# Layer norm statistics from VectorE's batch-norm instruction in a two-layer graph kernel

## The chip, the cores and the metric

The kernel runs on one core of a Trainium2 chip. The core has five engines that run side by side, each working through its own queue of instructions in order: TensorE (PE in the profile), VectorE (DVE), ScalarE (ACT), GpSimd (POOL) and SyncE (SP, which issues plain DMA transfers). They wait for one another through semaphores. The metric is the device time of one execution in microseconds (us), as the median of several runs.

## The reference

Sixteen graphs (B) of 1024 nodes (N) with 64 channels (C) each go through two layers. Each layer starts with a layer norm over the channels and a ReLU.

```python
def _layernorm(x, axis=-1, eps=1e-5):
    m = jnp.mean(x, axis=axis, keepdims=True)
    v = jnp.var(x, axis=axis, keepdims=True)
    return (x - m) / jnp.sqrt(v + eps)

# layer 0
h = jnp.maximum(_layernorm(x), 0.0)
x = x + matmul(adj / clip(sum(adj, 2), 1), h)
# layer 1
h = jnp.maximum(_layernorm(x), 0.0)
x = x + L1(h, adj, nodemask, W1, b1, W2, b2)
```

Layer 1 looks at the neighbours of every node (the nonzero entries of its row of `adj`), leaves out some of them in nodes with more than ten neighbours, takes three quantiles of the neighbours' values in each channel, adds their weighted sum to the node's own value, and sends the result through a small two-layer network of 128 hidden units.

## The kernel before

A batch is one graph. Its 1024 nodes lie as 8 row blocks (NT) of 128 partitions (P), so that a tensor of node features is a tile of 128 x 8 x 64.

The program is written by a planner that runs on the host while the instructions are issued. Each kind of work is a Python generator, called a stream. Before each step it yields the engine that it needs next and a function that says when its data will be there by the planner's own clocks. `Plan.run` takes the stream that can begin earliest (with a rank to put one before another) and lets it issue up to its next yield. `Plan.note` (line 271) advances the clocks: it prices a VectorE operation at 0.07 us plus 1.04 ns per element of the largest operand, a ScalarE operation at 0.06 us plus 0.86 ns per element, 0.11 us for each per-partition operand and 0.09 us for an accumulated output, and an indirect DMA at 1.27 us. So the order of instructions on every engine depends on the planner's prices, while the chip runs each engine's queue in that order, whatever the real times are. The margins SLACK (2 us), LOOSE (7 us) and LATE (14 us) keep a step from being put too early.

Layer 0 is made of eight streams (lines 560 to 809), each of which runs over the 16 batches:

- `loads` brings the node features `xt` and the rows `at` of the adjacency by SP's DMA queue; `signs` makes `sg`, the signs of a row block, on ScalarE, and `listing` takes the largest eight of four segments of them on VectorE (`rec`), which are the neighbour lists.
- `beginnings` (line 578) does the first layer norm: it calls `normed` (line 504) on `xt` and writes `h0`, the input of the products.
- `transposes` turns the adjacency on TensorE, and ScalarE copies it out (`att`); `products` multiplies it by `h0` and adds the residual on VectorE, which writes the layer's result into `row[:, :, X1:R0]`.
- `channels` (line 723) does the second layer norm: it calls `normed` on that part of `row`, writes the first 64 columns of `row`, and has SP store them in the table `tab`.
- `endings` sorts the nodes by their number of neighbours and scatters the records (`row`) to `srt` with eight indirect DMAs per batch, which GpSimd issues.

When the four batches of a group are done, `group` (line 1102) prepares the group's lists on VectorE, and jobs follow (`Job`, line 831): each gathers neighbours' rows from `tab` into `places` by indirect DMAs on GpSimd (four buffers), sorts them by min and max on VectorE, weights them on ScalarE and VectorE, sums and multiplies on TensorE, and scatters the result to the output, again from GpSimd. The jobs of the first three groups run in between layer 0 of later batches. After layer 0 come the last group and the jobs of the longest lists (`long_lists`, tiles `lplaces` and `long_other`).

`normed` is what the change touches. It takes `xt`, an input of 128 x 8 x 64. One VectorE reduction sums each row of 64, and one operation scales the eight sums to minus the mean (`s`). Then ScalarE squares each of the eight blocks with `s` as its bias, and the accumulated output of each square is a column of `v`, the sum of squared deviations. A yield stands before every second square (line 512), so other streams' ScalarE work can come between; another (line 517) puts VectorE's next step 2 us after the last square. VectorE scales `v` and adds epsilon, ScalarE takes the square root, VectorE the reciprocal and the product with `s`, and ScalarE applies scale, bias and ReLU to the eight blocks in `h`. A second path, `dense_path`, with its own `normed`, is taken only if the lists overflow.

Of the kernel before, what the change touches and what calls it, by code (L numbers as in the profile page):

```python
# [9 lines left out]
F32 = mybir.dt.float32  # L10
# [4 lines left out]
AF = mybir.ActivationFunctionType  # L15
OP = mybir.AluOpType
AX = mybir.AxisListType

P = 128
# [195 lines left out]
SLACK = 2.0  # L215
# [18 lines left out]
class Plan:  # L234
# [25 lines left out]
    def room(self, name, bufs):  # L260

        tiles = self.slots.get(name, ())
        if len(tiles) < bufs:
            return 0.0
        old = tiles[-bufs]
        return INF if self.users[old] else max(self.used.get(old, 0.0), self.ready.get(old, 0.0))

    def at(self, *tiles):
        return max(self.ready.get(t.tensor.name, INF) for t in tiles)
# [104 lines left out]
def list_path(ctx, tc, x, adj, nodemask, w1, b1, w2, b2, out, go):  # L374
    nc = tc.nc
    B, N, C = x.shape
    H = w1.shape[1]
    CO = w2.shape[1]
    NT = N // P
# [8 lines left out]
    X1 = W  # L388
    R0 = X1 + C
# [9 lines left out]
    tiny = ctx.enter_context(tc.tile_pool(name="tiny", bufs=2))  # L399
# [98 lines left out]
    nc = plan.nc  # L498
    new, free, room, at = plan.tile, plan.release, plan.room, plan.at
# [1 line left out]

    def normed(h, xt):

        s = new(tiny, [P, NT], F32, "ln_s", 4)
        nc.vector.tensor_reduce(s, xt, AX.X, OP.add)
        nc.vector.tensor_scalar(s, s, -1.0 / C, None, op0=OP.mult)
        v = new(tiny, [P, NT], F32, "ln_v", 4)
        for t in range(NT):  # L510
            if t % 2 == 0:
                yield "ACT", lambda: at(s)
            sq = new(tiny, [P, C], F32, "ln_sq", 2)
            nc.scalar.activation(
                sq, xt[:, t, :], AF.Square, bias=s[:, t:t + 1], accum_out=v[:, t:t + 1]
            )
        yield "DVE", lambda: at(v) + SLACK
        nc.vector.tensor_scalar(v, v, 1.0 / C, EPS, op0=OP.mult, op1=OP.add)
        yield "ACT", lambda: at(v) + SLACK
        nc.scalar.activation(v, v, AF.Sqrt)  # L520
        yield "DVE", lambda: at(v) + SLACK
        nc.vector.reciprocal(v, v)
        nc.vector.tensor_tensor(s, s, v, OP.mult)
        for t in range(NT):
            if t % 2 == 0:
                yield "ACT", lambda: at(s)
            nc.scalar.activation(
                h[:, t, :], xt[:, t, :], AF.Relu, bias=s[:, t:t + 1], scale=v[:, t:t + 1]
            )
# [26 lines left out]
    def known(st, *names):  # L556

        return max(at(st[name]) if name in st else INF for name in names)
# [19 lines left out]
    def beginnings(pool, now):  # L578

        for b, st in enumerate(batch):  # L580
            now[0] = b
            yield "DVE", lambda: max(known(st, "xt", "mrow"), room("h0", 3), room("row", 4))
            mrow_f = new(tiny, [NT, P], F32, "mrow_f", 2)
            nc.vector.tensor_copy(mrow_f, st["mrow"])

            h0 = new(pool, [P, NT, C + 1], F32, "h0", 3, users=2)
            nc.vector.memset(h0[:, :, C:], 1.0)
            row = st["row"] = new(pool, [P, NT, RW], F32, "row", 4, users=1)
            nc.vector.memset(row[:, :, C:W], -1.0)
            yield from normed(h0[:, :, :C], st["xt"])  # L590
            st["h0"] = h0
            yield "PE", lambda: max(at(mrow_f), room("ps_small", 3))
            pm = new(ps_s, [P, HALF], F32, "ps_small", 3, users=1)
            nc.tensor.transpose(pm[:, :NT], mrow_f, ident[:NT, :NT])
            yield "ACT", lambda: at(pm)
            nc.scalar.copy(row[:, :, RW - 1], pm[:, :NT])
            nc.scalar.copy(row[:, :, RW - 2], row_f)
            free(pm)
# [124 lines left out]
    def channels(pool, now):  # L723

        for b, st in enumerate(batch):
            now[0] = b
            row = lambda: st["row"]
            yield "DVE", lambda: known(st, "row") if st["residual"] == 2 else INF
            yield from normed(row()[:, :, :C], row()[:, :, X1:R0])
            g = max(g for g in range(NG) if FIRST[g] <= b)  # L730
            lo = (b - FIRST[g]) * TS
            nc.sync.dma_start(
                tabs[g][lo:lo + N, :].rearrange("(t p) w -> p t w", p=P), row()[:, :, :W]
            )
            st["normed"] = True
# [592 lines left out]
    with tc.tile_pool(name="lay0", bufs=2) as pool:  # L1328

        for stream, first in (  # L1330
            (endings, 0), (channels, 1), (products, 2), (transposes, 4), (listing, 5),
            (beginnings, 6), (loads, 7), (signs, -15),
        ):
            now = [0]
            plan.add(stream(pool, now), lambda first=first, now=now: 10 * now[0] + first)
        plan.run(lambda: progress["batches"] == B)
# [5 lines left out]
    nc = tc.nc  # L1342
# [291 lines left out]
```

## Time and profile before

| what | value |
|---|---|
| median of 3 runs | 1947.84 us (1942.62 to 1948.89) |
| span of the profiled execution, first to last instruction | 1511.0 us |
| mean granted TensorE clock in it | 0.699 of full speed |
| median less span | 436.8 us |
| DMA | 133.36 MB, mean 88 GB/s |
| ScalarE busy with the squares and their accumulator reads (`ln_sq`) | 34.02 us before 216 us, 55.91 us from there to 890 us |

The profile comes from one execution and gives the span alone; its whole time is not listed, so the difference to the median of other runs stands beside it. Busy time counts a moment once, even where two instructions of an engine overlap in the pipeline, so it is less than the count times the mean duration. "Idle before" is time in which an engine did nothing before an instruction of that group, and what ended it is named after an arrow. All instructions that the planner issues carry line 228 (its helper), so groups are told apart by the tile that they write: `ln_s`, `ln_v` and `ln_sq` are the layer norms, `row` the records, `srt` their scatter, `places` and `lplaces` the gathered neighbours, `y` and `out_dram` the output.

### The profile page before, as it was taken

The numbers are of one execution on the slowest core, as the hardware profiler recorded it, in microseconds if no ns is written. First come the engines' busy times: TensorE is split into PE (matmuls) and PEld (weight loads), VectorE is DVE, ScalarE is ACT, GpSimd is POOL, SyncE is SP. The second block draws the span as 40 slices with busy tenths as digits, with TensorE's granted clock in tenths as the row PEclk, the third lists the DMA queues.
The fourth block names the chain that finished last, engine by engine and source line by source line (L and its number), as shares of the span: only waits on it lengthen the run. The fifth ranks groups of instructions, "written<-read, shape, count | busy, mean of one in ns | idle before, by whom it ended". The sixth has DMA issues, their size and how long they took to land. (4 is left out here: it accounts for less than half of the span.)

```text
span 1511.0 us, 15983 instructions
## 1 busy us (share of the span) xinstructions
PE 738.8 (49%) x3192; PEld 464.7 (31%) x3192; DVE 1191.3 (79%) x4104; ACT 816.4 (54%) x2789; POOL 957.2 (63%) x1154
## 2 busy tenths in 40 slices
PE   4778777327877556567667620024000123228542
PEld 2434334214544233343444320012000122216432
DVE  6777798997899779859869869893059999986875
ACT  7989878557879457757975520201050223148341
POOL 0122227777678757757777787667777777765083
PEclk8889888658888777869688755555555565558765
DMA  5445665424355253355341242111111111211010
GB/s 177 150 142 168 163 210 160 123 73 114 101 162 152 59 174 94 99 126 161 94 140 31 60 101 68 50 37 28 30 26 23 28 28 40 44 33 22 2 25 13
DMA packets 135718, 133.36 MB, mean 88 GB/s; under 512 B 100756, under 2 KB 103444, under 8 KB 135492
## 3 DMA queue, kind: packets, MB, share of 16 engines
q1 hardware_dynamic: 102876, 90.79, 20.8%
q0 software_dynamic: 32736, 41.47, 11.2%
q14 instruction: 78, 0.64, 0.1%
q8 instruction: 28, 0.46, 0.1%
HBM read 112.90 MB, written 23.61 MB: 90 GB/s over the span
## 5 line engine op out<-in xcount | busy, mean ns | idle before, releaser
L228 POOL DMA_INDIRECT places<-tab,idx x372 | 370.2, 995 | 131.7 <-issue 101.8
L228 PE MATMUL pt<-ident,prod 128*128 128x128 f32 (+1 forms) x736 | 160.2, 377 | 517.8 <-DVE prod L228 241.2
L228 PEld LDWEIGHTS pt<-ident,prod 128*128 128x128 f32 (+1 forms) x736 | 129.3, 256 | 550.4 <-ACT prod L228 412.4
L228 PE MATMUL ps_small<-att,h 128*65 128x512 f32 x512 | 254.7, 644 | 27.3 <-ACT h L228 10.5
L228 POOL DMA_INDIRECT srt<-row,to x128 | 125.9, 984 | 165.8 <-ACT row L228 144.0
L228 PE MATMUL pt<-ident,at 128*128 128x128 f32 x1024 | 176.7, 320 | 96.0 <-ACT att L228 71.1
L228 POOL DMA_INDIRECT lplaces<-whole,lidx x163 | 167.2, 1026 | 55.6 <-issue 48.5
L228 DVE MAX8 rec<-sg 128x8 f16<-128x256 f16 x512 | 180.1, 414 | 4.4
L228 PEld LDWEIGHTS pt<-ident,at 128*128 128x128 f32 x1024 | 136.9, 164 | 143.5 <-ACT att L228 93.8
L228 ACT ACTIVATE sg<-at 128x1024 f16<-128x1024 f32 x128 | 134.8, 1054 | 75.0 <-DMA at<-in_adj_dram 65.7
L228 ACT COPY att<-pt 128x512 f32<-128x512 f32 x256 | 141.9, 582 | 20.7 <-PE pt L228 18.8
L228 POOL DMA_INDIRECT places<-tab,last_idx x124 | 123.8, 998 | 41.3 <-issue 35.0
L228 PEld LDWEIGHTS ps_small<-att,h 128*65 128x65 f32 x512 | 74.7, 151 | 161.9 <-issue 123.2
L228 ACT ACTIVATE places<-places,gone 128x64 f32<-128x64 f32 x496 | 123.5, 335 | 0.5
L228 ACT ACTIVATE prod<-places,w 128x64 f32<-128x64 f32 x213 | 54.1, 336 | 120.5 <-DVE w L228 120.5
L228 POOL DMA_INDIRECT out_dram<-y,nodes_i x93 | 91.8, 987 | 22.6 <-issue 15.1
L228 DVE TENSOR_TENSOR sg<-sg,keyed 128x1024 f16<-128x1024 f16 x128 | 87.2, 681 | 23.7 <-ACT sg L228 23.7
L228 ACT ACTIVATE gone<-gone 128x15 f32<-128x15 f32 (+9 forms) x40 | 8.2, 206 | 169.2 <-DVE ok L228 169.0
L228 DVE TENSOR_TENSOR long_other<-lplaces 128x512 f32<-128x512 f32 (+5 forms) x124 | 64.1, 555 | 29.1 <-ACT lplaces L228 28.9
L228 DVE TENSOR_TENSOR other<-places,other 128x64 f32<-128x64 f32 (+6 forms) x204 | 69.6, 341 | 5.9
L228 PE MATMUL ps_small<-ot,w_sb 128*128 128x128 f32 (+3 forms) x112 | 47.6, 513 | 44.2 <-DVE y L228 31.2
L228 DVE TENSOR_TENSOR places<-places,other 128x64 f32<-128x64 f32 (+2 forms) x208 | 62.3, 309 | 4.9
(231 smaller groups left out, 1670.8 us busy)
## 6 DMA issues: line engine op xcount, KB each, us to landing
at<-in_adj_dram SPq DMA_DIRECT2D x128, 512.0 KB
places<-tab,idx POOLq DMA_INDIRECT x372, 2.5
whole<-tab SPq DMA_DIRECT2D x4, 1057.0 KB
tab<-row SPq DMA_DIRECT2D x16, 264.0 KB
xt<-in_x_dram SPq DMA_DIRECT2D x16, 256.0 KB
lplaces<-whole,lidx POOLq DMA_INDIRECT x163, 2.4
srt<-row,to POOLq DMA_INDIRECT x128, 2.7
places<-tab,last_idx POOLq DMA_INDIRECT x124, 2.4
```

What stands on the lines that cost most here:

```text
L228: ins = getattr(self._engine, op)(*args, **kwargs)
```

## The change

`normed` gets a switch `stats`, and both calls in layer 0 set it. With it, eight `bn_stats` instructions on VectorE, one for each block of 64 elements, write six numbers each: count, mean and sum of squared deviations of the elements with even index, and the same of those with odd index. Five further VectorE operations on 128 x 8 elements put the halves together: the difference of the two means (`apart`), their sum (`s`), the sum of the two squared deviations (`v`), then C/4 times the square of the difference, which is added to `v`. Minus one half times `s` is then minus the mean. The reduction, the eight squares on ScalarE, the yields before them and the yield after them are not issued on this path. From the scaling of `v` on nothing changes. `dense_path` is unchanged.

```diff
--- before.py
+++ after.py
@@ -501,20 +501,34 @@
 
 
 
-    def normed(h, xt):
+    def normed(h, xt, stats=False):
 
         s = new(tiny, [P, NT], F32, "ln_s", 4)
-        nc.vector.tensor_reduce(s, xt, AX.X, OP.add)
-        nc.vector.tensor_scalar(s, s, -1.0 / C, None, op0=OP.mult)
         v = new(tiny, [P, NT], F32, "ln_v", 4)
-        for t in range(NT):
-            if t % 2 == 0:
-                yield "ACT", lambda: at(s)
-            sq = new(tiny, [P, C], F32, "ln_sq", 2)
-            nc.scalar.activation(
-                sq, xt[:, t, :], AF.Square, bias=s[:, t:t + 1], accum_out=v[:, t:t + 1]
-            )
-        yield "DVE", lambda: at(v) + SLACK
+        if stats:
+            st = new(tiny, [P, NT, 6], F32, "ln_st", 2)
+            for t in range(NT):
+                nc.vector.bn_stats(out=st[:, t, :], in_=xt[:, t, :])
+            apart = new(tiny, [P, NT], F32, "ln_apart", 2)
+            nc.vector.tensor_tensor(apart, st[:, :, 1], st[:, :, 4], OP.subtract)
+            nc.vector.tensor_tensor(s, st[:, :, 1], st[:, :, 4], OP.add)
+            nc.vector.tensor_tensor(v, st[:, :, 2], st[:, :, 5], OP.add)
+            nc.vector.scalar_tensor_tensor(
+                apart, apart, float(C) / 4.0, apart, op0=OP.mult, op1=OP.mult
+            )
+            nc.vector.tensor_tensor(v, v, apart, OP.add)
+            nc.vector.tensor_scalar(s, s, -0.5, None, op0=OP.mult)
+        else:
+            nc.vector.tensor_reduce(s, xt, AX.X, OP.add)
+            nc.vector.tensor_scalar(s, s, -1.0 / C, None, op0=OP.mult)
+            for t in range(NT):
+                if t % 2 == 0:
+                    yield "ACT", lambda: at(s)
+                sq = new(tiny, [P, C], F32, "ln_sq", 2)
+                nc.scalar.activation(
+                    sq, xt[:, t, :], AF.Square, bias=s[:, t:t + 1], accum_out=v[:, t:t + 1]
+                )
+            yield "DVE", lambda: at(v) + SLACK
         nc.vector.tensor_scalar(v, v, 1.0 / C, EPS, op0=OP.mult, op1=OP.add)
         yield "ACT", lambda: at(v) + SLACK
         nc.scalar.activation(v, v, AF.Sqrt)
@@ -587,7 +601,7 @@
             nc.vector.memset(h0[:, :, C:], 1.0)
             row = st["row"] = new(pool, [P, NT, RW], F32, "row", 4, users=1)
             nc.vector.memset(row[:, :, C:W], -1.0)
-            yield from normed(h0[:, :, :C], st["xt"])
+            yield from normed(h0[:, :, :C], st["xt"], True)
             st["h0"] = h0
             yield "PE", lambda: max(at(mrow_f), room("ps_small", 3))
             pm = new(ps_s, [P, HALF], F32, "ps_small", 3, users=1)
@@ -726,7 +740,7 @@
             now[0] = b
             row = lambda: st["row"]
             yield "DVE", lambda: known(st, "row") if st["residual"] == 2 else INF
-            yield from normed(row()[:, :, :C], row()[:, :, X1:R0])
+            yield from normed(row()[:, :, :C], row()[:, :, X1:R0], True)
             g = max(g for g in range(NG) if FIRST[g] <= b)
             lo = (b - FIRST[g]) * TS
             nc.sync.dma_start(
```

## The prediction

> **What bounds the kernel now.** I read five views in this order: the page's busy shares and slices, the busy time in four stretches, the waits of GpSimd, the groups by shape on ScalarE, and the timeline of VectorE for durations. The page first:
>
> ```profile
> PE 738.8 (49%) x3192; PEld 464.7 (31%) x3192; DVE 1191.3 (79%) x4104; ACT 816.4 (54%) x2789; POOL 957.2 (63%) x1154
> ...
> DVE  6777798997899779859869869893059999986875
> ACT  7989878557879457757975520201050223148341
> POOL 0122227777678757757777787667777777765083
> ```
>
> By shares VectorE (DVE) looks like the bound, and the change loads it further. But the GpSimd row stays at 6 to 8 tenths from the sixth slice to the 36th, and that is a full queue: between two gathers lie 0.30 us that the waits view calls "issue", so a 0.99 us gather takes a 1.25 to 1.3 us turn. The stretches and GpSimd's waits in the first two of them:
>
> ```profile
> 0.00:216.00 216.00, 161.44 (x646) 83.54 (x646) 165.78 (x598) 183.94 (x560) 40.31 (x76) 0.87 0.54 164
> 216.00:890.00 674.00, 421.01 (x1759) 259.61 (x1760) 561.66 (x1955) 465.71 (x1574) 498.33 (x617) 0.75 0.41 114
> 890.00:1170.00 280.00, 31.18 (x121) 20.78 (x119) 183.57 (x609) 43.43 (x167) 210.32 (x224) 0.52 0.19 44
> 1170.00:1511.00 341.00, 125.20 (x668) 100.75 (x668) 280.30 (x944) 123.35 (x488) 208.22 (x239) 0.63 0.12 26
> ```
> ```profile
> POOL srt L228 <- ACT row L228: 134.7, 8, 63.7
> POOL tab L228 <- DVE deg L228: 17.3, 1, 17.3
> POOL gat_rows L228 <- DVE nodes_i L228: 16.3, 1, 16.3
> ```
> ```profile
> POOL places L228 <- issue: 87.8, 288, 0.3
> POOL gat_rows L228 <- DVE y L228: 12.3, 1, 12.3
> ```
>
> The columns of a stretch are its length, busy time of PE, PE's loads, DVE, ACT and POOL, the clock, the DMA share and GB/s. The reader is to see two regimes. Up to 216 us GpSimd starves: it waits 134.7 us for the ScalarE writes into `row`, then 34 us for the preparation of the first group. ScalarE is the busiest engine there (184 of 216 us). From 216 us GpSimd works through its queue with hardly a stop: in the next 674 us its real waits (12.3, 9.2, 7.1, 5.6 and a few of 2 us) make some 40 us. From 890 to 1170 us it waits some 10 us in all, and VectorE stands idle for 48.9 us at one go waiting for the gathers of the longest list. Only after 1170 us does it wait much again:
>
> ```profile
> POOL out_dram L228 <- DVE y L228: 58.1, 5, 36.2
> ```
>
> So the time is the moment at which GpSimd gets its first group, plus its queue, plus what it still waits.
>
> [...] the turn (start to start of operations that don't depend on each other): 29 maxima of 32 elements take 2.77 us, so (2.77 - 0.18)/28 = 92 ns[...]; the duration shown for one is some 85 ns longer, which a dependent one waits out. [...]
>
> **The change part by part**, per call of `normed` (32 calls: 16 batches times two norms).
>
> Removed from ScalarE: eight squares and their accumulator reads.
>
> ```profile
> L228 ACT ACTIVATE ln_sq<-xt,ln_s 128x64 f32<-128x64 f32 x128 | 42.8, 341 | 4.3 <-DVE ln_s L228 4.3
> ...
> L228 ACT ACTIVATE ln_sq<-row,ln_s 128x64 f32<-128x64 f32 x128 | 42.5, 334 | 11.9 <-DVE ln_s L228 11.9
> ```
>
> The reads overlap the squares (pairs follow at 0.33 us), and the windows of `ln_sq` have 34.0 us before 216 us, 55.9 after, together 89.9: 2.8 us per call.
>
> Removed from VectorE: the sum and its wait.
>
> ```profile
> 53.64 0.69 DVE L228 TENSOR_REDUCE ln_s<-row 128x8 f32<-128x512 f32 x1
> 54.36 0.17 DVE L228 TENSOR_SCALAR ln_s<-ln_s 128x8 f32<-128x8 f32 x1
> ```
>
> That is 0.72 us to the dependent scaling, which is 0.08 more to the next independent one; the scaling itself comes back with another factor.
>
> Added to VectorE: eight statistics of 64 elements. No row shows one. [...] I take 0.127[...]. Then, after 0.1 us for the dependence, five 8-element operations and the scaling: three independent at 0.08, two more links of the chain at 0.20 and 0.08, the scaling 0.08: 0.6 us. Together 1.7 us for 0.8: +0.9 us per call, +28 us in all, 11 in the first stretch (12 calls have their `ln_v` there) and 18 in the second. With dear statistics +2.7 us per call, +86 us.
>
> Moved: the wait of VectorE for the squares goes (3.9 us in the first stretch, 5.3 in the second), and one trip VectorE-ScalarE-VectorE per call. In the first batch the second norm runs from 53.64 to the first ReLU at 66.99, of which the squares take 57.6 to 61.5; the square root then stands behind a copy. The 14 operations leave in one piece, with nothing of another stream between: what is queued behind them on VectorE (mostly a sign product with four maxima, 2.1 us) is late by 1.7 us at most, and those waiting for it have buffers ahead (4 of `sg`). The planner prices a statistic at 0.07 + 64 x 0.00104 = 0.137 us, close to my value, so its order fits the engines as well as before. No DMA is added or moved in itself; the `row` scatters (8 on GpSimd) and the table store on SP follow their producer.
>
> *First stretch.* Between 60 and 180 us ScalarE is busy 107.7 of 120 us, TensorE 90, VectorE 88; batches follow at 32.8, 34.5 and 33.2 us (first `row` scatters at 67.7, 100.5, 135.0, 168.2). Two calls a batch take 5.6 us from ScalarE and give VectorE 1.8. ScalarE would then need some 25 us a batch, VectorE 26, TensorE 25, and none can be packed without gaps: I take 30 to 31, so 3 us for each of three batches. The first batch gains some 4 us through four calls less before it, and the preparation of the first group, on VectorE from 177 to 213 us, loses 2. That is 3 x 3 + 4 - 2 = 11, say 12 with the shorter trip of the last second norm. Bounds: 0, if DMA (0.54 busy) and TensorE keep the pace, to 20, all of the 34 us less 14 for VectorE and the gaps.
>
> *Second stretch.* VectorE gets 18 us and loses 10.2 us of waits inside the norms; its other waits for ScalarE (18.0 for gathered rows, 13.4 for signs) get shorter as ScalarE loses 56 us. I cost this at nothing: it is hidden under GpSimd's queue. Without that cover it would be up to 18 us.
>
> *The rest.* The code is the same, the stretch to 1170 us has 49 us of slack on VectorE, but the planner's order can differ.
>
> Sum: span 1511.0 - 12 = 1499. The page doesn't list the profiled execution's whole time; the median of the three runs lies 436.8 us above the span, and I leave that as it is: 1936.
>
> **Rivals.**
> *Nothing measurable (1944 to 1953, take 1947).* The start is earlier, but GpSimd runs into later `row`s and waits it out, or the end is set by the last long list on VectorE. For it: VectorE is busy for 192 of the 200 us from 1150. Against: GpSimd hardly waits between 216 and 1170.
> *The last drain turns out worse (slower, take 1960).* Near the end a scatter waits 36.2 us for `y` while the 20 gathers of the last long list stand behind it on GpSimd; they start at 1434 us and all that follows waits for them. The planner puts scatters and gathers in order by its own clocks, which the change shifts (ScalarE 2.5 us less per call, VectorE 0.9 more). If one more wait of this kind stands ahead of a long list's gathers, it costs 25 to 35 us; with the 12 gained, +12 to +20. It decides from a wait of some 20 us. For it: the tail has 58 us of such waits. Against: the same luck can take one away, to 1910.
> *Dear statistics (slower, take 1965).* At 0.35 us or more each, VectorE needs +54 us in the second stretch; 112 of its 674 us aren't busy, 73 of that in named waits, of which half can't go. It becomes the bound from some +35 us on; then the start's gain is gone too: about +17.
>
> **How the numbers follow.** Earlier start 0.50, nothing 0.16, worse drain 0.20, dear statistics 0.14. About 0.3%, 5.8 us, can be told from no change. Faster 0.50, same 0.16, slower 0.34. The likeliest case alone runs from 1920 (20 at the start and a kinder drain) to 1942. The range has to reach into both slower rivals: 1912 to 1968.
>
> **What would show it.** Right: no squares, ScalarE at about 727 us busy, VectorE near 1220, statistics at about 0.21 us each with a turn near 0.13; the first `tab` scatter some 12 us before 213; GpSimd's waits between there and 1170 unchanged near 50 us. Wrong: a turn of the statistics over 0.3 us; the first group no earlier; new GpSimd waits for `row` or for `places` on VectorE; or an end in which the long lists' gathers stand behind other waits.

## The result, and the profile after

The changed kernel takes 1949.4 us (median of 19 runs, 1936.2 to 1960.6), the kernel before takes 1950.9 us in as many runs beside it (1942.6 to 1957.7). The ratio is 0.9989 with a 95% interval of 0.9969 to 1.0008: no change that can be measured. The forecast was 1936 us; what came is the rival "nothing measurable".

One thing has to be known to read the numbers below. The same program ran in two lengths: the kernel before took about 1515 us in some sessions and about 1950 to 1980 us in others, on one and the same chip within half an hour, and never anything in between. The profile that the prediction argued from (span 1511.0 us) is of the short kind; all 19 + 19 timed runs of the result are of the long kind, and so is the profile of the changed kernel. Its span is 1942.5 us and the time of that same execution 1944.27 us, so the time around a span is some 2 us, not the 436.8 us that the prediction carried along. To compare like with like, the kernel before was profiled again in a long session (`b_again`, span 1954.5 us).

First the page of the changed kernel: busy time, share of the span and instructions, then the busy tenths in 40 slices.

```profile
PE 785.2 (40%) x3192; PEld 491.9 (25%) x3192; DVE 1219.7 (63%) x4487; ACT 748.1 (39%) x2295; POOL 943.1 (49%) x1155
...
DVE  7989649556643675774555738940025987646764
ACT  7786526254246453524652301001410142136341
POOL 0231662634652356475454456675773036573163
```

The work changed as foreseen: `b_again` has 1193.5 us for VectorE and 830.3 for ScalarE, so VectorE got 26.2 us more and ScalarE 82.2 less. But the GpSimd row, which stood at 5 to 8 tenths in the short profile from its seventh slice to its 37th, now swings between 2 and 7, with one slice at 0 and one at 1, and after the start no engine stays full: VectorE reaches 9 tenths in three slices, the others in none.

The statistics by tile in the changed kernel (duration in ns as min/median/max), and the timeline of VectorE in its first norm (start, length, operation):

```profile
L228 DVE BATCH_NORM_STATS2 ln_st<-xt x128: 193/197/229, 7.8 to 966.8; 128x6 f32<-128x64 f32 x128
L228 DVE BATCH_NORM_STATS2 ln_st<-row x128: 207/211/227, 58.6 to 1109.1; 128x6 f32<-128x64 f32 x128
```
```profile
7.78 1.07 DVE L228 BATCH_NORM_STATS2 ln_st<-xt 128x6 f32<-128x64 f32 x8
8.89 0.17 DVE L228 TENSOR_TENSOR ln_apart<-ln_st 128x8 f32<-128x8 f32 x1
...
9.54 0.17 DVE L228 TENSOR_SCALAR ln_v<-ln_v 128x8 f32<-128x8 f32 x1
```

Eight statistics take 1.07 us, and from the first of them to the scaling of `ln_v` it is 9.54 - 7.78 = 1.76 us, against the 1.7 of the prediction. The 0.35 us each of the rival "dear statistics" were a supposition of the author's; measured are 0.20 and 0.21 us for one, with a turn of (1.07 - 0.20)/7 = 0.124 us.

Now the stretches, with the same columns as before. The first two of the changed kernel, then the same of `b_again`:

```profile
0.00:216.00 216.00, 167.10 (x704) 90.46 (x704) 189.94 (x777) 167.09 (x396) 53.82 (x93) 0.89 0.63 187
216.00:890.00 674.00, 299.93 (x1166) 179.35 (x1166) 417.79 (x1598) 288.14 (x861) 351.48 (x431) 0.67 0.33 86
```
```profile
0.00:216.00 216.00, 152.49 (x586) 78.96 (x587) 153.37 (x565) 178.44 (x547) 38.25 (x73) 0.84 0.53 155
216.00:890.00 674.00, 339.80 (x1308) 207.05 (x1306) 410.65 (x1430) 340.66 (x1118) 346.85 (x430) 0.67 0.34 90
```

In the first stretch the changed kernel does more of everything but ScalarE (704 matmuls against 586), so the start is quicker. In the second GpSimd is busy for 351 and 347 of 674 us in both, where the short profile had 498. The sentence "GpSimd works through its queue with hardly a stop" is true of the short kind and false of the kind that was timed.

What GpSimd waits for up to 230 us, in the changed kernel and in `b_again` (total, times, longest):

```profile
POOL srt L228 <- ACT row L228: 120.8, 9, 63.9
POOL tab L228 <- DVE ln_v L228: 17.4, 1, 17.4
POOL gat_rows L228 <- DMA at<-in_adj_dram: 13.0, 1, 13.0
```
```profile
POOL srt L228 <- ACT row L228: 145.7, 8, 64.4
POOL gat_rows L228 <- DVE nodes_i L228: 18.2, 1, 18.2
POOL tab L228 <- DVE deg L228: 17.3, 1, 17.3
```

The wait for ScalarE's writes into `row` is 25 us shorter. The first `tab` scatter comes at 196 us in place of 226.

That lead doesn't last. A scatter of some batch is a poor mark of it, as the planner put layer 0's steps earlier in GpSimd's queue (its last `srt` is the 508th indirect DMA in place of the 523rd) and pushed jobs back. A fairer mark is how many indirect DMAs GpSimd has issued, whichever they are (the order differs, so the nth is not the same one in both); 931 in all. From the starts of those instructions in the traces, us from the start of the span:

| kernel, kind of session | 101st | 201st | 301st | 501st | 701st | 886th | last |
|---|---|---|---|---|---|---|---|
| before, short (profile of the prediction) | 301 | 441 | 581 | 860 | 1126 | 1382 | 1502 |
| before (`b_again`), long | 340 | 541 | 736 | 1106 | 1425 | 1800 | 1946 |
| changed, long | 301 | 519 | 734 | 1112 | 1412 | 1806 | 1933 |

39 us ahead after 100, 22 after 200, 2 after 300, 13 ahead once more at the 701st, 6 behind at the 886th (the last before the final drain). These are single traces: a second one of the changed kernel in another long session (`a_again`) is up to 15 us later at these marks, so differences of 10 us say little, while the 39 us at the 101st stand clear (301 us again). Only the drain gives 19 us back: 127 us from there to the last DMA in place of 146.

What the long kind looks like from inside, `b_again`, timeline of all engines (start, length, instruction, and in brackets the idle time before it with what ended it):

```profile
578.89 3.78 PE L228 MATMUL pt<-ident,prod 128*128 128x128 f32 x16 [3.28 <-remote]
...
588.06 0.17 DVE L228 TENSOR_TENSOR w<-wu 128x10 f32<-128x10 f32 x1
588.08 0.19 ACT L228 ACTIVATION_READ_ACCUMULATOR sg<-at 128x1 f32 x1
588.39 0.99 POOL L228 DMA_INDIRECT srt<-row,to  x1 [0.30 <-issue]
...
595.75 0.17 DVE L228 SCALAR_TENSOR_TENSOR w<-wu,w 128x10 f32<-128x10 f32 x1 [7.52 <-issue]
...
616.11 0.95 POOL L228 DMA_INDIRECT places<-tab,idx  x1 [0.30 <-issue]
617.36 0.94 POOL L228 DMA_INDIRECT places<-tab,idx  x1 [0.30 <-issue]
618.84 0.37 ACT L228 COPY ot<-pt 128x256 f32<-128x256 f32 x1 [30.57 <-remote]
618.94 0.33 DVE L228 MEMSET prod<- 128x320 f32 x1 [23.02 <-remote]
...
619.26 1.22 PE L228 MATMUL ps_small<-ot,w_sb 128*128 128x256 f32 x2 [36.59 <-issue]
```

GpSimd issues 45 indirect DMAs in one row, from 561 to 618.3 us. ScalarE, VectorE and TensorE work on for a dozen of them, then creep, then stand still, and all three go on within one microsecond of the row's end. `w<-wu,w` at 595.75 reads what VectorE itself had written one instruction earlier, and yet it starts 7.5 us after it.

What they wait for stands in the trace's record of semaphore updates. ScalarE's `ot<-pt` at 618.84 waits for the semaphore that TensorE posts; TensorE's last matmul before it had ended at 578.89 + 3.78 = 582.67 us, but the update that lets ScalarE go is recorded at 618.82, 36 us later. The same update is the last of those that VectorE's `prod` at 618.94 waits for, and TensorE's next matmul waits for ScalarE's `ot`. The step at 595.75 waits for VectorE's own semaphore, whose update is recorded at 594.31, 6 us after the instruction before it had ended. The label "remote" says only that no instruction ended shortly before the update, not that the cause lies outside the core. Over whole traces, the updates of TensorE's semaphore:

| kernel, kind | instructions that post it | updates recorded | of these over 5 us after the latest post | longest delay, us |
|---|---|---|---|---|
| before, short | 675 | 675 | 0 | 4.9 |
| before (`b_again`), long | 675 | 587 | 56 | 36.1 |
| changed, long | 664 | 577 | 35 | 28.9 |

So in the long kind updates reach the waiting engines late, and the engines stand still for want of them. (The long traces also hold fewer updates; whether some came together or weren't recorded can't be told.)

Over the whole trace, the share of time in which VectorE was busy while GpSimd issued, by the place of the DMA in its row (a row: DMAs less than 0.7 us apart; the DMAs' own durations, without the gaps between them):

| kernel, kind | 1st to 8th | 9th to 16th | 17th to 24th | 25th to 32nd | later |
|---|---|---|---|---|---|
| before, short | 0.76 | 0.89 | 0.88 | 0.69 | 0.77 |
| before (`b_again`), long | 0.77 | 0.63 | 0.36 | 0.18 | 0.10 |
| changed, long | 0.81 | 0.66 | 0.30 | 0.12 | 0.29 |

So in the long kind a row of indirect DMAs and the other engines' work largely take turns; in the short kind they overlap. From 213 us to the end of the span GpSimd is without a DMA (gaps of a microsecond and more) for 131 us in the short profile, 605 in `b_again` and 603 in the changed kernel. VectorE and GpSimd are not slower at their own work: a maximum takes 414 ns on average in the pages of both kinds, a gather 995 ns in the short one and 961 in the long (977 in the changed kernel). TensorE is a little (a transpose of the adjacency 320 and 342 ns, at a mean granted clock of 0.699 and 0.642; 336 ns at 0.652 in the changed kernel), but its busy time grows by 60 us only, of the span's 443. Nor do transfers take much longer: the packets of SP's queue fill 20.8% of the short span and 16.7% of the long one, 314 and 326 us if all 16 DMA engines are taken together.

The waits of the whole changed kernel show the same (total, times, longest):

```profile
ACT ot L228 <- remote: 123.5, 9, 29.6
...
ACT att L228 <- remote: 87.4, 13, 18.8
...
ACT prod L228 <- remote: 71.7, 3, 56.4
```

In the short profile no wait of any engine is put down to "remote".

### The profile page after: what moved, and what is told of

The parts are those of the page before. It is cut to its first block, busy times and chain, and to the rows that moved or that the text cites. A ratio compares the mean times of both kernels' runs of the same rounds, so it can differ in the third digit from the quotient of the medians.

```text
span 1942.5 us, 15899 instructions
## 1 busy us (share of the span) xinstructions
PE 785.2 (40%) x3192; PEld 491.9 (25%) x3192; DVE 1219.7 (63%) x4487; ACT 748.1 (39%) x2295; POOL 943.1 (49%) x1155
## 4 chain that ended last, share of the span: by engine, by line
DVE 29%; issue 15%; another core or an unknown queue 13%; ACT 12%; PE 9%; POOL 6%; DMA 2%; DVEq 0%; SPq 0%; POOLq 0%; ACTq 0%
PE pt L228 6%; DVE other L228 5%; DVE places L228 4%; POOL places L228 4%; PE ps_small L228 4%; ACT places L228 3%; ACT lplaces L228 3%; DVE lplaces L228 3%; DVE rec L228 3%; DVE long_other L228 2%; ACT sg L228 1%; ACT prod L228 1%; DVE sg L228 1%; ACT att L228 1%
## 5 line engine op out<-in xcount | busy, mean ns | idle before, releaser
L228 POOL DMA_INDIRECT places<-tab,idx x372 | 363.6, 977 | 242.9 <-issue 107.3
L228 PE MATMUL ps_small<-att,h 128*65 128x512 f32 x512 | 258.8, 657 | 68.0 <-DVE y L228 26.4
L228 PE MATMUL pt<-ident,at 128*128 128x128 f32 x1024 | 189.2, 336 | 176.9 <-ACT att L228 72.9
L228 PEld LDWEIGHTS pt<-ident,at 128*128 128x128 f32 x1024 | 146.2, 173 | 226.2 <-ACT att L228 94.5
L228 POOL DMA_INDIRECT lplaces<-whole,lidx x163 | 157.8, 968 | 56.9 <-issue 48.5
L228 ACT COPY ot<-pt 128x128 f32<-128x128 f32 (+3 forms) x56 | 22.1, 398 | 249.9 <-remote 123.5
L228 ACT ACTIVATE prod<-places,w 128x64 f32<-128x64 f32 x231 | 58.8, 336 | 133.1 <-remote 71.7
L228 PE MATMUL ps_small<-ot,w_sb 128*128 128x128 f32 (+3 forms) x112 | 55.5, 590 | 96.7 <-ACT ot L228 51.2
```

The lines of the kernel that those rows point to most:

```text
L228: ins = getattr(self._engine, op)(*args, **kwargs)
```

## The experiments

Each ratio is to the kernel before, run beside it on the same chip. Lead theory at first: the gain of the start is real and is lost later; the rivals differ in what loses it.

**`b_again`: the kernel before, unaltered.**

> The kernel before, unchanged, profiled once more and timed against itself. Theory A (the profile that the prediction was argued from shows a lighter execution than the timed ones: its span is 1511.0 us where the times are 1950, while the span after the change, 1942.5, is as long as the times): this span is near 1940 and shows ScalarE and VectorE standing still for 5 to 30 us at a time while GpSimd issues rows of gathers. Rival (436 us lie outside the instructions before the change, and the change brought them inside): the span is near 1511 again. Both: ratio 1.000 within 0.003.

1954.3 us, ratio 1.0005 (0.9984 to 1.0026), span 1954.5 us. It is the yardstick of the long kind used above: the 437 us between the first span and the times are inside the execution, not around it.

**`new_work_old_order` and `new_work_old_order_2`: the statistics, with GpSimd's and VectorE's queues ordered as before.** The planner is told the old instructions while the new ones are issued, and the old yields stay. The traces show that this keeps the order of GpSimd and VectorE, but not that of the other queues: of the 3192 matmuls 413 stand at another place than in `b_again`, of ScalarE's 1987 common instructions 489. Why isn't known.

```diff
+            raw.bn_stats(out=st[:, t, :], in_=xt[:, t, :])
...
+        plan.note("DVE", "tensor_reduce", (s, xt, AX.X, OP.add), {})
...
-            nc.scalar.activation(
-                sq, xt[:, t, :], AF.Square, bias=s[:, t:t + 1], accum_out=v[:, t:t + 1]
-            )
+            plan.note(
+                "ACT", "activation", (sq, xt[:, t, :], AF.Square),
+                {"bias": s[:, t:t + 1], "accum_out": v[:, t:t + 1]},
+            )
```

> The batch-norm statistics as in the change, but the planner is told the prices of the sums and squares and yields where they yielded, so that GpSimd's queue has exactly the order of before. Theory A (the freed ScalarE time falls into standstills of ScalarE): no faster than the changed kernel, ratio to before 0.996 to 1.002. Theory B (the earlier start of the first group is real, and the new order gives it back later): faster, 0.988 to 0.994, 12 to 23 us. Theory C (VectorE's added 28 us give it back): 0.998 to 1.003.

> The statistics on VectorE, but with the planner told the old prices, so that every queue has the order of before. In the 1515 kind of session: theory (the start is what gains, and it gains through the planner's earlier places for the scatters of the first batches as much as through ScalarE's freed time; with the old order the first group comes 8 to 14 us earlier only if ScalarE's freed time alone does it): ratio 0.990 to 0.998, first scatter of the first group's lists at 200 to 210 us. Rival (the new order is what gains): ratio 0.998 to 1.005. In the 1950 kind it measured 1.005, and the same again is expected.

Both fell into long sessions: 1.0051 (1.0032 to 1.0070) and 1.0047 (1.0030 to 1.0065). The first is outside all three ranges expected, nearest to Theory C. The statistics in this order cost 9 to 10 us there. By GpSimd's count the first is 13 us ahead of `b_again` at the 101st DMA and 3 behind at the 886th: 16 us given back on the way (the second 12 ahead and 11 or 12 behind, against the `b_again` of another session). That is close to the 18 us that VectorE gets in the second stretch, which the prediction had named as the cost without GpSimd's cover; since TensorE's and ScalarE's order changed too, it isn't shown that VectorE's work is the cause. The drain has the same length as before (146 us), so the drain's 19 us in the changed kernel come from its new order.

**`old_work_new_order`: sums and squares, with the planner told the new prices.** GpSimd's queue is that of the changed kernel.

```diff
+        raw.tensor_reduce(s, xt, AX.X, OP.add)
...
+            act.activation(
...
-        yield "DVE", lambda: at(v) + SLACK
+        for t in range(NT):
+            plan.note("DVE", "bn_stats", (), {"out": st[:, t, :], "in_": xt[:, t, :]})
```

> The sums and squares of before, but the planner is told the prices of the statistics, so that GpSimd's queue has exactly the order of the changed kernel. Theory A: ratio to before 0.998 to 1.004. Theory B: slower, 1.005 to 1.012, as it has the cost of the new order without the gain. Theory C: 0.995 to 1.000, as it has none of the added VectorE work.

2015.1 us, ratio 1.0312 (1.0280 to 1.0344). It doesn't isolate the order: VectorE's next step now stands directly behind the squares, and VectorE waits for them 27 times, 177 us in all. As a measure of the order's cost it is of no use; it shows what a step costs that is placed without the wait that it has. One thing can be read from it: its drain is 131 us, near the changed kernel's 127, so the shorter drain goes with the new order, not with the statistics.

**`first_only`: statistics in the first norm of each batch, sums and squares in the second.**

The edit is against the changed kernel:

```diff
-            yield from normed(row()[:, :, :C], row()[:, :, X1:R0], True)
+            yield from normed(row()[:, :, :C], row()[:, :, X1:R0])
```

> Only the first norm (of xt) uses the statistics; the second keeps sums and squares. Theory A and C: within 0.3% of before. Theory B: anywhere within 1% of before, since the order is a third one; if the time moves by over 0.4% here while both norms together move by 0.1%, the order matters more than the work.

1984.2 us, ratio 1.0139 (1.0099 to 1.0180). No theory had expected more than 1%; Theory B's sign, over 0.4% here while the whole change moves the time by 0.1%, is there. Half the change costs more than the whole. Less work is added to VectorE than in the full change, so VectorE's added work alone can't be the reason; the planner's order is another one again. Most likely this is what an order is worth here by chance: more than one per cent.

**`b_pause8` and `a_pause8`: before and changed, each with GpSimd stopped for a moment ahead of every 8th gather.** The planner isn't told, so all other queues stay.

```diff
     def gather(dst, src, idx):
+        count[0] += 1
+        if count[0] % 8 == 0:
+            for _ in range(12):
+                nc.gpsimd._engine.memset(stop, 0.0)
```

> The kernel before; ahead of every eighth gather GpSimd also clears a small tile of its own twelve times (one to three microseconds, some 87 times), which the planner isn't told, so every other queue is as before. Theory A (while GpSimd issues gathers back to back, the other engines' waits are not answered, and they stand still until the row of gathers ends): the pauses let them on, the share of time in gathers in which no other engine works falls from 0.29 to under 0.15, and the time falls by over 3%. Rival (GpSimd's queue is the bound and the standstills have another cause): the pauses add their own 100 to 200 us in part, the time rises by 2% or more. If GpSimd has slack, as its 605 us outside DMAs say, and the standstills are not tied to rows of gathers: within 1%.

> The changed kernel with the same pauses. Theory A: as b_pause8, and with the standstills gone the change's gain shows: faster than b_pause8 by 0.5 to 2%. Rivals: as b_pause8, and within 0.5% of it.

The runs fell in a short session (before 1515.6 us). `b_pause8` took 1660.0 us, ratio 1.0957 (1.0934 to 1.0980), `a_pause8` 1639.8, ratio 1.0821 (1.0800 to 1.0843). The 83 pauses hold GpSimd for 204 us in the trace, more than I had reckoned, and 144 of them reach the end. So in the short kind GpSimd's queue is the bound, as the prediction had it, if with some slack. And the change gains 20 us there, within Theory A's range, though with hardly a standstill to remove it says nothing for that theory. By GpSimd's count it is 26 us ahead at the 101st DMA (291 against 317), 9 at the 886th, 24 at the end: even there most of the start's lead was gone before the drain, which is 15 us shorter.

**`b_slack15` and `a_slack15`: before and changed with the planner's margin at 1.5 us.**

```diff
-SLACK = 2.0
+SLACK = 1.5
```

> The kernel before with the planner's margin SLACK at 1.5 us in place of 2: the same instructions in another order. Theory B (the order that the planner happens to find is worth as much as the change): the time moves by over 0.5% either way. Rival (the order hardly matters): within 0.3% of before.

> The changed kernel with SLACK at 1.5 us. Theory B: its ratio to b_slack15 differs from the 0.9989 of the pair at 2 us by over 0.5%. Theory C (the gain at the start is given back by VectorE's added work whatever the order): the same ratio, 0.996 to 1.002.

Same short session: 1530.3 us, ratio 1.0095 (1.0070 to 1.0121), and 1492.8 us, ratio 0.9855 (0.9832 to 0.9878). So the order alone moves the kernel before by 1%, as Theory B has it. With this margin the change gains 37 us (ratio of the two 0.976, far from 0.9989, though that was measured in long sessions), and `a_slack15` beats the kernel before. Of the 44 us between the two profiles' last DMAs, 17 are there at the 886th, 27 come in the drain (105.5 us in place of 132.4).

**`a_again`, `b_pause8_2`, `a_slack15_2`: the changed kernel, the pauses and the smaller margin once more.**

> The changed kernel, unaltered, in a session of its own, beside the kernel before. Two kinds of sessions have been seen: in one the kernel before takes about 1515 us (its first profile, and the last four runs), in the other about 1950 us. Theory (in the 1515 kind GpSimd's queue is the bound, and the earlier start of the first group, 12 to 25 us, goes through to the end): ratio to before 0.98 to 0.99 there, first scatter of the first group's lists at 190 to 203 us against 213. In the 1950 kind: 0.997 to 1.001, as measured. Rival (the gain is lost in the tail of layer 1 in either kind, because the planner's order there is a worse one): ratio 0.995 to 1.003 in the 1515 kind too.

> The kernel before with 12 small GpSimd memsets ahead of every 8th gather, which keep GpSimd from issuing for some 140 us in all. In the 1515 kind of session they cost 144 us, as much as they take. In the 1950 kind: theory (there all other engines stand still while GpSimd issues a long row of indirect DMAs, and go on when the row ends; the pauses break the rows up): less than half of the 140 us is paid, ratio at most 1.035, and the time in which nothing but GpSimd works falls from 246 us to below 180. Rival (the standstills have to do with the bytes or the number of DMAs, not with the rows): the pauses come on top, ratio 1.06 to 1.08. Rival (GpSimd's queue has some 600 us of waits there and hides the pauses): ratio 1.00 to 1.02, with the standstills as long as before.

> The changed kernel with the planner's margin SLACK at 1.5 us in place of 2. In the 1515 kind of session it took 0.9855 of the time of before. In the 1950 kind: theory (margins are shorter, so more steps are placed before their data are there; but all engines wait for something else there, so little changes): ratio 0.99 to 1.005. Rival (the smaller margin suits the new order in either kind): 0.98 to 0.99. Rival (a step placed too early holds up its queue longer there, as semaphores take longer): 1.01 to 1.03.

The runs fell in a long session (before 1951.8 us). `a_again`: ratio 1.0022 (1.0003 to 1.0042), the result again, a little above the 0.997 to 1.001 expected. `a_slack15_2`: 1.0088 (1.0056 to 1.0119), so it beats the kernel before in the short kind alone; its partner `b_slack15` was not run in a long session. `b_pause8_2`: 1727.2 us, ratio 0.8863 (0.8831 to 0.8895). Stopping GpSimd for 212 us made the kernel 224 us quicker. None of the three expectations of this run had a gain in it; Theory A of `b_pause8` had (over 3%). The two rivals fall; what the theory set as its limits holds (ratio at most 1.035, standstills below 180 us), though it took the relief for a part of the price and not for more than it. In the trace of `b_pause8_2` the time in which a gather is issued and no other engine computes falls from 207 us in `b_again` to 72 (the 246 of the expectation was reckoned more loosely), GpSimd's time without a DMA, pauses included, from 605 to 368, and the updates of TensorE's semaphore that come over 5 us late from 56 to 22, the longest delay from 36.1 to 18.9 us. A pause in the timeline of its GpSimd:

```profile
562.42 0.95 POOL L228 DMA_INDIRECT places<-tab,idx  x1 [0.30 <-issue]
563.36 2.47 POOL L819 MEMSET stop<- 128x64 f32 x12
566.41 0.95 POOL L228 DMA_INDIRECT places<-tab,idx  x1 [0.58 <-ACT att L228]
```

From the end of one DMA to the start of the next it is 3.0 us, where the gaps beside it have 0.3. The scatters are not broken up by this edit, and in rows that stay long VectorE still falls to 0.15 from the 17th DMA on.

**`a_pause8_2`, `b_short8`, `b_pause16`, `b_pause4`: what part of the pause matters.** The diff is that of `b_pause4` against `b_pause8`; `b_short8` has 8 and 3 there, `b_pause16` 16 and 12, and `a_pause8_2` is `a_pause8` again.

```diff
-        if count[0] % 8 == 0:
-            for _ in range(12):
+        if count[0] % 4 == 0:
+            for _ in range(6):
```

> The changed kernel with the pauses of 12 memsets ahead of every 8th gather, once more. Where the kernel before takes 1950 us, the kernel before with the same pauses took 1727. Theory (the standstills of all engines during long rows of indirect DMAs ate the change's gain; without them GpSimd's queue is the bound again and the earlier start comes through, as it did where before takes 1515 us, by 20 us): 1695 to 1715, ratio to before 0.868 to 0.880. Rival (the gain is lost in the planner's order of the last jobs, with or without standstills): 1722 to 1735, ratio 0.882 to 0.889. Where before takes 1515 us: 1640 again, ratio 1.082.

> The kernel before with only 3 memsets (some 0.5 us) ahead of every 8th gather, in place of 12 (some 2.5 us). Theory (a row's length is what matters: any break lets the other engines' semaphores through): as much relief as with 12 and less cost, 1600 to 1690 where before takes 1950, ratio 0.82 to 0.87. Rival [...]: most of the standstills stay, ratio 0.94 to 0.99. Where before takes 1515 us: it costs 30 to 50 us, ratio 1.02 to 1.035.

> The kernel before with 12 memsets ahead of every 16th gather, so rows of twice the length at half the total pause (some 70 us). In a row of 45 indirect DMAs of the kernel before, VectorE, ScalarE and TensorE went on for about 15 of them and then stopped. Theory (a standstill begins only some 14 to 16 indirect DMAs into a row): nearly as much relief as every 8th and half the cost, ratio 0.85 to 0.89 where before takes 1950. Rival (standstills grow in proportion to the row): ratio 0.92 to 0.96. Where before takes 1515 us: ratio 1.04 to 1.055.

> The kernel before with 6 memsets ahead of every 4th gather: rows of half the length, each pause half as long, the same total. Theory (row length decides): relief as with every 8th or more, ratio 0.86 to 0.89 where before takes 1950. Rival (length of the pause decides): ratio 0.92 to 0.97. Where before takes 1515 us: ratio 1.08 to 1.11.

The session was short (before 1514.2 us), so these runs say nothing of the standstills: whether the length of a pause or that of a row brings the relief stays open. They do give the price of GpSimd's time in the short kind:

| kernel | GpSimd held, us (trace) | time lost, us | ratio |
|---|---|---|---|
| `b_short8` | 49 | 18 | 1.0139 (1.0117 to 1.0161) |
| `b_pause16` | 102 | 59 | 1.0404 (1.0381 to 1.0426) |
| `b_pause4` | 202 | 140 | 1.0943 (1.0920 to 1.0966) |

From 49 to 102 us held, (59 - 18)/(102 - 49) = 0.8 of each microsecond reaches the end; carried on below 49 us, this line would leave the first 25 or so free, an estimate. `b_short8` costs less than the 30 to 50 us expected, the other two lie at or in their ranges. `a_pause8_2` repeats `a_pause8`: 1.0841 (1.0822 to 1.0859).

**`a_again_2` and `a_pause8_3`.**

> The changed kernel, unaltered, once more. Where the kernel before takes about 1515 us: theory (GpSimd's queue is the bound, so the earlier start comes through: a_pause8 is 20 us under b_pause8, a_slack15 37 us under b_slack15): 1485 to 1503 us, ratio 0.98 to 0.993, first scatter of the first group's lists at 190 to 203 us. Rival (the planner's order of the last jobs gives the gain back): ratio 0.995 to 1.003. Where before takes 1950 us: 1.000 to 1.003, as twice before.

> The changed kernel with the pauses of 12 memsets ahead of every 8th gather. Where the kernel before takes 1950 us (with the same pauses 1727): theory (the standstills ate the change's gain): 1695 to 1715, ratio to before 0.868 to 0.880. Rival (the order of the last jobs ate it): 1722 to 1735, ratio 0.882 to 0.889. Where before takes 1515 us: 1640 for the third time, ratio 1.083.

The session was long (before 1979.6 us). `a_again_2`: 1.0014 (0.9988 to 1.0040). `a_pause8_3`: 0.8767 (0.8716 to 0.8817), against 0.8863 (0.8831 to 0.8895) for the kernel before with the same pauses in the other long session. The ratio is in the range of the theory that the standstills ate the gain, but a gain of some 1% isn't shown by it: the two ran on different chips in different sessions, where the kernel before took 1979.6 and 1951.8 us, and in its own time `a_pause8_3` is the slower, 1740.0 us against 1727.2. Nor does the trace bear that theory out as to the start: at the 301st DMA `a_pause8_3` stands at 655 us and `b_pause8_2` at 651, at the 886th at 1618 and 1588, so the start's lead is gone there too. What is left is the drain: 109 us in place of 124.

The drain is the one place where every pair agrees. GpSimd's waits after the 886th DMA, `b_again` and then the changed kernel:

```profile
POOL out_dram L228 <- DVE y L228: 78.1, 3, 36.3
```
```profile
POOL out_dram L228 <- DVE idle L228: 33.4, 1, 33.4
POOL out_dram L228 <- DVE y L228: 22.0, 2, 18.3
```

78.1 us of waits become 55.4. Ahead of the last long list two scatters stand in the opposite order: they wait 16.0 and 36.3 us in `b_again`, 33.4 and 3.7 in the changed kernel; behind it the wait is 25.9 and 18.3.

Versions that beat both kernels: in long sessions the changed kernel with pauses (0.877) and the one before with them (0.886); in short ones `a_slack15` (0.986). None of these does in both kinds: the pauses cost 8 to 10% in the short one, the smaller margin 0.9% in the long one.

## Why the prediction was wrong

*The step that failed: "I cost this at nothing: it is hidden under GpSimd's queue".* With it the 12 us of the start were carried to the end unchanged. In the timed kind that cover isn't there: GpSimd is without a DMA for 605 us after the start in place of 131, and a lead of 39 us at the 101st DMA was 2 us at the 301st. The cover was believed in because of "the median of the three runs lies 436.8 us above the span, and I leave that as it is": this took the profile as a picture of the timed executions, and the rest as something around it. It was inside: the timed executions are of the other kind, with a span 2 us below their time. So "From 216 us GpSimd works through its queue with hardly a stop" is false of them, and with it the sum of first group, queue and waits. The hint was there before any run: the profile held nothing that could be the missing 437 us. That the forecast would have come true in the short kind isn't shown either: there the paused pair lost 17 of its 26 us between the 101st and the 886th DMA.

*The statistics: right.* The turn (start to start of operations that don't depend on each other) is 0.124 us by the first norm. The 0.127 was an estimate of the author's; the maxima of the profile before lead to nearly the same:

```profile
199.02 2.77 DVE L228 MAX8 keys<-recs 128x8 f32<-128x32 f32 x29
11.87 1.41 DVE L228 MAX8 rec<-sg 128x8 f16<-128x256 f16 x4
```

With 0.18 us for one of the first kind and 0.41 for one of the second the turns are (2.77 - 0.18)/28 = 0.092 us at 32 elements and (1.41 - 0.41)/3 = 0.333 at 256, and a straight line between the two has 0.126 at 64, an estimate, as the second kind reads fp16. VectorE's busy time rose by 26.2 us against 28, with the end at 1219.7 against "near 1220". ScalarE lost 82.2 us against 89.9: the squares and their reads are 91.8 us of `b_again`, but the planner gave ScalarE 18 products more in the changed order (`prod<-places,w`, 213 to 231, 3.7 us), and what is left overlaps less.

*The first stretch: right in kind, too small.* Forecast 12 us earlier, 0 to 20. Measured at the first `tab` scatter: 30 us between the long profiles (226 to 196), 26 between the paused short ones (215 to 189), 11 with the smaller margin (211 to 200). The step that was off is the pace of a batch: I took 30 to 31 us in place of 33.5; the changed kernel has 26, 31 and 29, and the kernel before in the long kind 33, 38 and 40 (in the paused short pair 21, 31, 29 and 33, 35, 33). `new_work_old_order` is only 10 us ahead at that mark (216), so some 20 of the 30 come with the planner's new order, with earlier places for these scatters, which the prediction hadn't counted. A smaller slip of reading: the GpSimd row of the profile stands at 6 to 8 tenths from the seventh slice on, not the sixth, and two of its slices up to the 36th are at 5.

*The second stretch: what ate the lead.* The price given for the case without cover, up to 18 us, is near what `new_work_old_order` lost (16). That this is VectorE's added work is a likely reading and not shown; no run took that work away by itself.

*The rivals.* "Nothing measurable" came about, but no run shows its reason, a wait for later `row`s or the last long list; what they show is that an overlap of the profile is missing in the timed executions. That the end came out so near zero is luck: a lost lead and a kinder drain of about the same size. "The last drain turns out worse" has the right place and the wrong sign: the same luck of the order made the drain shorter, by 15 to 27 us in each pair. "Dear statistics" is refuted: 0.124 us of turn, against a limit of 0.3 in the prediction.

*What stays open.* The unaltered change was never run in a short session; the two altered pairs gained 1.2% and 2.4% there. What makes a session long or short isn't known. Nor is what makes the semaphore updates late (by up to 36.1 us in `b_again`, 28.9 in the changed kernel): that they are late is shown, the reason isn't. And the long kind loses some 45 us between the 101st and the 886th DMA, of which the added VectorE work may be 16 to 18; the rest belongs to the new order, and which of its steps wasn't found out.

## What to carry to other kernels

Lay the span of a profile beside the measured times before you argue from it: where they are much further apart than the 2 us seen here, the profile may show another kind of execution than the timed one, and its bound may not be theirs. Measure a lead by how far the bounding queue has got (its nth instruction) rather than by when some batch reaches a mark, since a planner can bring the mark forward without any work being done sooner. And where a hand-made planner sets the order, an edit of a few microseconds can come with a new order worth a per cent (here 1.0% slower with the smaller margin, 1.4% with the statistics in the first norm alone): run the new work in the old order before you credit the work, and see in its trace whether every queue did keep that order.

## What the runs showed of the hardware that was not expected

- One program, two lengths: 1515 and 1950 us, both on the same chip within half an hour, each within 1.5% through a session.
- In the long kind the other engines stand still during rows of indirect DMAs: VectorE's busy share falls from 0.77 in the first eight of a row to 0.10 after the 32nd. With the same instructions in the short kind it stays between 0.69 and 0.89.
- The engines wait there for semaphore updates that come late: 56 of TensorE's are recorded over 5 us after its latest post, one 36.1 us after; in the short profile none. What delays them isn't known.
- There, 83 pauses of 2.6 us on GpSimd made the kernel 224 us quicker (ratio 0.886); in the short kind the same pauses cost 144 us.
- Eight batch-norm statistics of 64 fp32 elements take 1.07 us on VectorE, a turn of 0.124 us each in the first norm; in the second they take 1.10 us, a turn of (1.10 - 0.21)/7 = 0.127 us. Maxima of 32 elements had 0.092.
